# Alternating tiles of one and two experts, later masked adds, one select for two heads, and two buffer pools at the end

## The chip, the cores and the metric

The kernel runs on one core of a Trainium2 chip. Its time is the device time of one execution in microseconds (us). Three executions of the kernel before took 1357.25, 1357.31 and 1363.54 us, so the median is 1357.31 us. A fourth execution was recorded by the profiler; it took 1360.14 us, of which 1358.3 us lie between its first and its last instruction (its span).

The engines are named as in the profile: PE is the matrix engine (TensorE), DVE is VectorE, ACT is ScalarE, POOL is GpSimd and SP is SyncE, which here does nothing but start transfers (DMAs). Each engine has its own queue of instructions and takes them strictly in their order.

## The reference

The input is 2048 rows of 512 numbers. What is computed, in float32, is

```python
xn = layernorm(x)
out = x + attention(xn) + ffn(xn)

# attention: 16 heads, two score maps each (32 maps of width 16), rotary q and k
s = einsum('bthd,bshd->bhts', q, k) * scale      # causal
a = softmax(where(mask, s, -1e30))
attn = irfft((rfft(a1 @ v) - lam * rfft(a2 @ v)) * filt)   # a Gaussian filter along the rows
attn = rms_norm(attn per head) * (1 - LAMBDA_INIT) @ Wout

# ffn: 8 experts of width 352, the best two for every row, and a shared expert of width 704
y_all = einsum('eti,eih->eth', silu(h) * g, w2)
ffn = sum(y_all[topk] * topk_w) + silu(x @ sw1) * (x @ sw3) @ sw2
```

Both softmax maps are divided by their own sums before the second is subtracted from the first. The filter runs over all 2048 rows, so it can start in earnest only when the attention of every row is there.

## The kernel before, in words

**Stages.** From 0 to about 235 us: layer norm, q, k, v, the gate and the routing. From 235 to 600 us: attention, with the shared expert's products strewn in between. From 600 to about 1240 us: attention, with the routed experts' tiles strewn in between. From 1240 us: `ending()`, which applies the filter as matrix products, normalizes, projects with Wout, adds up and stores.

**Order.** In the attention stage all five engines run in the order in which the program writes the instructions; in `ending()` all but SP do. Nothing is rearranged by a scheduler. So the place of a line in the program is its place in its engine's queue.

**Attention.** Heads are taken in 8 groups g of two. In a group the four blocks of 512 queries are taken from the last, qc=3, to the first, qc=0; such a block of a group is a `Chunk`. A chunk's units (up to 512 columns of both maps of one head against 128 keys) go through `scores` (PE, L822, into `ps_s`), the exponential (ACT, L835, into one of 8 buffers `pt`), for units on the diagonal a causal select (POOL, L840), `values` (PE, L862, into `ps_o`), and `added` (DVE, a copy at L876 for the first unit of a head and adds at L879 after that), which keeps the running sums `sum0` and `sum1`. The units that hold diagonal blocks are called masked; the qc=0 chunk has masked units only, five of them, which give two copies and six adds. Four units make one iteration of the loop at L1029; a group has 17 iterations, of some 7.1 us each.

When the last values of a chunk are through, it is `closing`. In the next iteration PE first computes its row sums from `sum0` and `sum1` (`ps_sum`, L888), then transposes its outputs and its sums (`ps_ot` L900, `ps_st` L901), and DVE takes the reciprocals (`rcp`, L903 and L906) and multiplies (`o_n`, L908). An iteration later POOL writes the difference of the two maps into `vd` (L917). `folded` (L922 to L970) prepares a finished group for the filter in some thirty small adds, on POOL for all groups but the last, on DVE for the last one.

On DVE an iteration writes, in this order: the reciprocals and `o_n` of a chunk that closes, the copies and adds of unmasked units among the iteration's first two, the work on the experts' side mixed with one add at a time of the other two, and at last the adds of the iteration's masked units.

**Experts.** The rows sent to the 8 experts are cut into tiles of 128 rows, 34 of which run here. 28 tiles (numbers 0 to 27, `NP`) belong to one expert, 6 tiles (28 to 33) hold 64 rows each of two experts. `experts()` is a generator; each `work()` of the loop above lets it write one piece. For a tile it writes: `xT` (the rows transposed, L165), the first half of the up product with tanh (`xh`, L180, L190, L191), the second half (`xg`, L180, L197), the hidden rows turned back (`ps_u` L206, `uT` L208 and L209) and the down product (`xy`, L216), stored to `ys` at L228. There are two places for an expert's weights, `w_sb[0]` and `w_sb[1]`, each with an up part `wu` (1408 KB) and a down part `wd` (768 KB). Halves of tiles are counted by n, and the half n uses place n % 2; a tile of one expert takes one place, a tile of two experts takes both. When `xg` of a tile is written, SP starts the transfer of the up weights for two halves later into the places that this frees, and behind `xy` likewise for the down weights. After the last tile come the weights of the shared expert (`wex[NX]`, `wex[NX + 1]`), which the last 128 rows still need: `wh<-kept` at L246 and `wy` at L284.

**The end.** `ending()` takes its buffers from the pool `tp` (two of each kind), which lies where pools of the attention stage lay before. Among them are `ws` (L256, the shared expert's hidden values), `res` (12 buffers, loaded with the input's rows, to which POOL's DMA queue adds the shared and the routed outputs by accumulating transfers), `diff`, `first`, and `y_sb`, through which the shared expert's last output goes to `ysh[15]`. Its order on PE: the `wh` products, `ps_r` (L1141, from `vd`), the `ps_z` products (L1141), then 16 times transposes (L1262) and projection (L1270).

Of the kernel before, what the change touches and what calls it, by code (L numbers as in the profile page):

```python
# [19 lines left out]
P = 128  # L20
# [25 lines left out]
NR = NS - 2  # L46

NP = (T * TOP // HALF - NX) // 2
WUP = NE * 2 * FI
WCOL = WUP + NF * E  # L50
CONVS = 23
# [16 lines left out]
def block_kernel(  # L68
# [527 lines left out]
    def middle(general):  # L596


        with ExitStack() as pools:
# [29 lines left out]
            def experts():  # L629
# [45 lines left out]
                xT, late = transposed(xr.pop(0)), None  # L675
                yield 0.6

                sets = [[j] if j < NP else [2 * j - NP, 2 * j - NP + 1] for j in range(NR)]
                halves = [2 * j + i for j in range(NR) for i in range(len(sets[j]))]

                def places(j, part):
                    return [w_sb[n % 2][part] for n in sets[j]]

                def tile_down(j, uT):
                    return places(j, 1), uT, ys[j * P : (j + 1) * P, :], wcol[:, j : j + 1]

                for j in range(NR):
                    if j > 0:
                        late = tile_down(j - 1, turned_back(u))
                    half = up_first(places(j, 0), xT)  # L690
                    yield 2.9 if late else 2.4
                    u = up_third(places(j, 0), xT, half)
                    if j + 2 < NR:
                        xr.append(rows_of(j + 2))
                    for n in sets[j]:

                        m = n + 2 - len(halves)
                        es.append(routed(halves[n + 2]) if m < 0 else wex[NX + m : NX + m + 1])
                        fetch_up(es[n + 2], n % 2, nc.sync)
                    yield 2.4  # L700
                    if j + 1 < NR:
                        xT = transposed(xr.pop(0))
                    if late:
                        down(*late)
                        for n in sets[j - 1]:
                            fetch_down(es[n + 2], n % 2, nc.sync)
                    if j == 1:
                        shared.append(True)
                    if late:
                        yield 3.2  # L710
# [46 lines left out]
            def greatest(g, qc):  # L757
# [28 lines left out]
                nc.vector.tensor_copy(shift, ps.rearrange("p t q -> p (t q)"))  # L786
                return shift

            class Chunk:


# [19 lines left out]
                def scores(self, unit):  # L811

                    g, qc = self.g, self.qc
                    if general and not self.probs:
                        self.shift = greatest(g, qc)
                    ps = sps.tile([P, 2, QC], F32, tag="sc", name="ps_s")
                    for h, kb, off, col, w in unit:
                        for s in range(2):
                            r = slice(64 * s, 64 * s + 64)
                            k = keys[2 * g + h, kb // TQ][r, kb % TQ * P : (kb % TQ + 1) * P]  # L820
                            to = ps[:, s, col : col + w]
                            nc.tensor.matmul(  # L822
                                to, k, queries[2 * g + h, qc][r, off : off + w], start=True, stop=not general
                            )
                            if general:
                                r = 64 * h + 32 * s
                                nc.tensor.matmul(
                                    to, ones[r : r + 1, :], self.shift[r : r + 1, off : off + w],
                                    start=False, stop=kb < qc * TQ,
                                )  # L830
                                if kb >= qc * TQ:
                                    nc.tensor.matmul(to[:, :P], identb, mask, start=False, stop=True)
                    pt = pp.tile([P, 2, QC], F32, tag="pt", name="pt")
                    used = slice(min(c for *_, c, _ in unit), max(c + w for *_, c, w in unit))
                    nc.scalar.activation(pt[:, :, used], ps[:, :, used], AF.Exp, scale=SCALE)  # L835
                    for _, kb, _, col, _ in unit:
                        if kb >= qc * TQ and not general:

                            part = pt[:, :, col : col + P]
                            nc.gpsimd.affine_select(  # L840
                                out=part, in_=part, pattern=[[0, 2], [1, P]], compare_op=ALU.is_ge, fill=0.0,
                                base=0, channel_multiplier=-1,
                            )
                    ready = []
                    for h, kb, off, col, w in unit:
                        self.probs[h, kb] = pt[:, :, col : col + w], off
                        if (1 - h, kb) in self.probs:
                            ready.append((self, kb))
                    return ready
# [134 lines left out]
            for c in range(NQC):  # L984
                load_keys(0, c)
                if c == 0:
                    load_queries(0, NQC - 1)
            worked, begun, summed, held = 0.0, -1, 0, []
            todo, closing, closed, shared, ready, folding = [], [], [], [], [], None

            def burst(units):
# [21 lines left out]
            def work():  # L1013
                nonlocal worked
                worked += next(ex, work_all)

            def masked(entry):
                _, c, unit = entry
                return any(kb >= c.qc * TQ for _, kb, *_ in unit)

            def added(entries):

# [6 lines left out]
            for i in range(0, len(stream), 4):  # L1029
                units = stream[i : i + 4]  # L1030
                found = burst(units[:2])
                n, ended = values()
                for c in closing:
                    c.sums()
                    summed += 1
                if n < 2 and not closing:

                    work()
                found += burst(units[2:])
                while todo:  # L1040
                    ended += values()[1]
                todo += found
                for c in closed:
                    c.put(nc.gpsimd)
                    if c.qc == 0:
                        ready.append(c.g)
                closed, closing = closing, ended
                for c in closed:
                    c.finish()
                held, before = [], held  # L1050
                added(before)
                added(u for u in units[:2] if not masked(u))
                later = [u for u in units[2:] if not masked(u)]
                while True:
                    work()
                    added(later[:1])
                    later = later[1:]
                    if worked / (work_all - left) >= (i + 4) / len(stream):
                        break
                added(later)  # L1060
                added(u for u in units if masked(u))
                if any(map(masked, units)) or not shared:
                    steps = 0
                else:
                    steps = 1 if any(map(masked, stream[i + 4 : i + 8])) else 2
                for _ in range(steps):
                    if folding is None and ready:
                        folding = folded(ready.pop(0), nc.gpsimd)
                    if folding is not None and next(folding, 0) == 0:
                        folding = None  # L1070
            for c in closed:
                c.put(nc.gpsimd)
            ended = []
# [17 lines left out]
    def ending():  # L1091

        with tc.tile_pool(name="tail1", bufs=1) as t1, tc.tile_pool(name="tail", bufs=2) as tp, tc.tile_pool(
            name="tail_ps", bufs=4, space=PSUM
        ) as fps, tc.tile_pool(name="conv_ps", bufs=2, space=PSUM) as zps, tc.manual_schedule(
            engines={mybir.EngineType.PE, mybir.EngineType.DVE, mybir.EngineType.Activation, mybir.EngineType.Pool}
        ):
            conv = t1.tile([P, CONVS * P], F32, name="conv")  # L1100
            nc.scalar.dma_start(conv[:, : 11 * P], conv_t[:, : 11 * P])
            nc.scalar.dma_start(conv[:, 11 * P :], conv_t[:, 11 * P :])
            _, _, _, _, (_, _, stored), _ = expert(tp, fps)
            hidden, gated, times, _, result = shared_expert(tp, fps, 2)
            fetch_down(wex[NX + 1 : NX + 2], 1, nc.scalar)
            wo_sb = t1.tile([P, NE, E], F32, name="wo_sb")
            nc.scalar.dma_start(wo_sb, wout.rearrange("(c p) e -> p c e", p=P))
# [8 lines left out]

            def fetched(k, step):
                if step == 0:
                    res = tp.tile([P, E], F32, tag="res", name="res", bufs=12)
                    nc.sync.dma_start(res, query[0, order[k] * P : (order[k] + 1) * P, :])  # L1120
                    came.append(res)
                elif step == 1:
# [27 lines left out]
                return z  # L1150

            def copied(z):
                diff = tp.tile([P, 2, E], F32, tag="diff", name="diff")
                nc.scalar.copy(diff, z)
                return diff

# [23 lines left out]
            zr = pair("ps_r")  # L1180
            product(zr[:, 0, :], [(0, vd[:, 0, :])])
            product(zr[:, 1, :], [(1, vd[:, 1, :])])
            first = tp.tile([P, E], F32, tag="first", name="first", bufs=1)
            nc.scalar.copy(first, zr[:, 1, :])
            z4 = at(0, fold, 2)
            nc.vector.tensor_add(low[:, 0], zr[:, 0, :], first)
# [283 lines left out]
```

## Time and profile before

| what | value |
| --- | --- |
| three executions | 1357.25, 1357.31, 1363.54 us |
| profiled execution: time, span | 1360.14 us, 1358.3 us |
| mean clock granted to PE | 0.994 of full |
| PE busy | 1312.6 us (97% of the span) |
| DVE busy | 1005.4 us (74%) |
| ACT busy | 688.4 us (51%) |
| POOL busy | 626.3 us (46%) |
| PE busy in 235 to 600 us | 363.18 of 365 us |
| PE busy in 600 to 1240 us | 621.11 of 640 us |
| PE busy in 1240 to 1358.3 us | 103.97 of 118.3 us |

The profiled execution is 2.83 us longer than the median of the three others. 45.7 us of its span are without work on PE; 14 us of these lie behind 1240 us and 19 us between 600 and 1240 us. In the profile a name such as `xy<-wd,uT` tells what an instruction writes and reads; a bracket such as `[2.67 <-DMA wu<-in_wex_dram]` says that the engine had been idle for 2.67 us before the instruction and what ended the idle time.

### The profile page before, as it was taken

How to read it: one execution, taken by the hardware profiler on the slowest of the kernel's cores; microseconds unless marked ns; L12 is line 12 of the kernel's file. 1: busy time of each engine (PE TensorE's matmuls, PEld its weight loads, DVE VectorE, ACT ScalarE, POOL GpSimd, SP SyncE). 2: the span in 40 equal slices, each digit the busy share in tenths (PEclk: the TensorE clock that was granted, in tenths of full speed). 3: DMA queues.
4: the chain of work that ended last, by engine and by line, in shares of the span. 5: the costliest groups of instructions: out<-in, count | busy, mean ns of one | idle time of the engine just before them, and what ended most of it. 6: DMA issues, size and time to landing. Idle time of an engine off the chain costs nothing.

```text
span 1358.3 us, 20810 instructions
## 1 busy us (share of the span) xinstructions
PE 1312.6 (97%) x7554; PEld 600.3 (44%) x7554; DVE 1005.4 (74%) x1344; ACT 688.4 (51%) x847; POOL 626.3 (46%) x671
## 2 busy tenths in 40 slices
PE   7999999999999999999999999899999999987998
PEld 3444444334443444445444444344544444443544
DVE  7049883287668778868889986778898788764785
ACT  2311110265656566676666666566676666640221
POOL 0002330012221323235968984778589469421764
PEclk9999999999999999999999999999999999998999
DMA  9406673200211122235665656555565666777997
GB/s 375 171 16 171 201 196 97 89 15 32 75 43 31 40 75 82 74 123 170 190 194 143 226 176 180 181 173 174 185 194 178 210 189 230 262 294 293 175 219 169
DMA packets 75578, 214.29 MB, mean 158 GB/s; under 512 B 12244, under 2 KB 12696, under 8 KB 69576
## 3 DMA queue, kind: packets, MB, share of 16 engines
q1 hardware_dynamic: 62744, 185.68, 41.7%
q0 software_dynamic: 11056, 22.78, 8.6%
q10 hardware_dynamic: 1664, 4.38, 0.9%
q8 instruction: 63, 1.03, 0.3%
q14 instruction: 51, 0.42, 0.1%
HBM read 169.69 MB, written 43.10 MB: 157 GB/s over the span
## 4 chain that ended last, share of the span: by engine, by line
PE 65%; DVE 6%; POOL 5%; DMA 3%; issue 1%; ACT 1%; SPq 0%; DVEq 0%; ACTq 0%; POOLq 0%
PE ps_o L862 16%; PE ps_s L822 12%; PE wh L246 8%; PE xy L216 6%; PE xg L180 5%; PE xh L180 5%; PE wy L284 4%; PE ps_sum L888 2%; DMA wu<-in_wex_dram 2%; POOL pt L840 1%; PE po L1270 1%; DMA wd<-in_wex_dram 1%; DVE sum L879 1%; PE ps_ot L900 1%; PE ps_x L165 1%
## 5 line engine op out<-in xcount | busy, mean ns | idle before, releaser
L879 DVE TENSOR_TENSOR sum<-sum,pt 128x1024 f32<-128x1024 f32 (+3 forms) x576 | 621.4, 1128 | 36.3 <-ACT pt L835 21.6
L835 ACT ACTIVATE pt<-ps_s 128x1024 f32<-128x1024 f32 x544 | 527.3, 1023 | 184.3 <-PE ps_s L822 131.0
L840 POOL TENSOR_SCALAR_AFFINE_SELECT pt<-pt 128x256 f32<-128x256 f32 x256 | 171.0, 693 | 358.7 <-ACT pt L835 357.5
L862 PE MATMUL ps_o<-pt,vd 128*32 128x512 f32 (+3 forms) x2560 | 268.0, 534 | 4.1 <-POOL pt L840 4.1
L822 PE MATMUL ps_s<-qS,kS 64*128 64x512 f32 (+3 forms) x1280 | 203.8, 406 | 2.0 <-DVEq L1335 1.6
L822 PEld LDWEIGHTS ps_s<-qS,kS 64*128 64x128 f32 x1280 | 97.1, 185 | 177.0 <-issue 95.9
L246 PE MATMUL wh<-xnT,wu 128*128 128x512 f32 (+1 forms) x352 | 150.4, 574 | 0.0
L862 PEld LDWEIGHTS ps_o<-pt,vd 128*32 128x32 f32 x2560 | 66.9, 109 | 125.8 <-issue 103.5
L545 PE MATMUL ps_x<-xnT,wqk_sb 128*128 128x512 f32 x256 | 110.5, 593 | 0.0
L498 POOL DMA_INDIRECT who<-pairs,slot x32 | 33.1, 1034 | 165.9 <-DVE pairs L495 104.9
L216 PE MATMUL xy<-wd,uT 128*128 128x512 f32 (+3 forms) x240 | 97.1, 606 | 7.7 <-DVE rcp L903 6.3
L246 PEld LDWEIGHTS wh<-xnT,wu 128*128 128x128 f32 x352 | 64.1, 190 | 72.7 <-issue 56.5
L180 PE MATMUL xh<-wu,xT 128*128 128x352 f32 (+1 forms) x320 | 90.5, 473 | 4.2 <-DMA wu<-in_wex_dram 3.3
L917 POOL TENSOR_TENSOR vd<-o_n 128x128 f32<-128x128 f32 x60 | 62.2, 1057 | 65.6 <-DVE o_n L908 65.5
L180 PE MATMUL xg<-wu,xT 128*128 128x352 f32 (+1 forms) x320 | 88.6, 468 | 0.0
L545 PEld LDWEIGHTS ps_x<-xnT,wqk_sb 128*128 128x128 f32 x256 | 48.4, 190 | 60.6 <-issue 60.6
L284 PE MATMUL wy<-wd,ws 128*128 128x512 f32 x160 | 74.8, 603 | 0.0
L257 DVE SCALAR_TENSOR_TENSOR ws<-ws,wh 128x512 f32<-128x512 f32 (+4 forms) x26 | 16.7, 644 | 73.6 <-ACT ws L256 73.6
L1125 POOL DMA_INDIRECT res<-ys,slot x32 | 54.9, 1715 | 25.3 <-DMA res<-ysh 13.5
L562 ACT CAST hi<-turned 128x1024 fp32r<-128x1024 f32 x16 | 16.7, 1045 | 93.9 <-DVE turned L560 70.9
L180 PEld LDWEIGHTS xh<-wu,xT 128*128 128x128 f32 (+1 forms) x320 | 48.0, 176 | 31.7 <-issue 6.5
L180 PEld LDWEIGHTS xg<-wu,xT 128*128 128x128 f32 (+1 forms) x320 | 46.6, 174 | 34.4 <-issue 14.8
(254 smaller groups left out, 1416.8 us busy)
## 6 DMA issues: line engine op xcount, KB each, us to landing
wu<-in_wex_dram SPq DMA_DIRECT2D x44, 1408.0 KB
wd<-in_wex_dram SPq DMA_DIRECT2D x43, 768.0 KB
kS<-parts_k SPq DMA_DIRECT2D x128, 128.0 KB
qS<-parts_q SPq DMA_DIRECT2D x256, 64.0 KB
ys<-y_sb SPq DMA_DIRECT2D x34, 256.0 KB
parts_q<-hi SPq DMA_DIRECT2D x32, 256.0 KB
parts_k<-hi SPq DMA_DIRECT2D x16, 256.0 KB
parts_k<-turned SPq DMA_DIRECT2D x16, 256.0 KB
```

Source lines behind the costliest of these rows:

```text
L180: nc.tensor.matmul(dst[r, :], xT[:, c, r], w[:, o : o + FI], start=(c == 0), stop=(c == NE - 1), skip_group_check=True,)
L216: nc.tensor.matmul(y[r, :], uT[:m, ic, r], w[:m, ic * E : (ic + 1) * E], start=(ic == 0), stop=(ic == NF - 1), skip_group_check=True,)
L246: nc.tensor.matmul(dst, w_sb[o // WUP][0][:, o % WUP : o % WUP + P], x[:, c, :], start=(c == 0), stop=(c == NE - 1))
L284: nc.tensor.matmul(y, us[i][:, t * P : (t + 1) * P], w_sb[i // NF][1][:, i % NF * E : (i % NF + 1) * E], start=(i == 0), stop=(i == SCH - 1),)
L545: nc.tensor.matmul(ps[:, i, :], wqk_sb[st, qk][:, i, c, :], xnT[:, c, cols], start=(c == 0), stop=(c == NE - 1),)
L822: nc.tensor.matmul(to, k, queries[2 * g + h, qc][r, off : off + w], start=True, stop=not general)
L835: nc.scalar.activation(pt[:, :, used], ps[:, :, used], AF.Exp, scale=SCALE)
L840: nc.gpsimd.affine_select(out=part, in_=part, pattern=[[0, 2], [1, P]], compare_op=ALU.is_ge, fill=0.0, base=0, channel_multiplier=-1,)
L862: nc.tensor.matmul(self.o[r : r + 32, off:], vd[:, kb, v0 : v0 + 32], pt[:, s, :], start=first, stop=self.ended, skip_group_check=True,)
L879: nc.vector.tensor_add(to, to, pt)
L917: eng.tensor_add(vd[:, self.qc * TQ : (self.qc + 1) * TQ, v0 : v0 + 32], self.o_n[:, :, h, 0, :], self.o_n[:, :, h, 1, :],)
L1125: nc.gpsimd.indirect_dma_start(out=came[k], out_offset=None, in_=ys, in_offset=bass.IndirectOffsetOnAxis(ap=slot[:, step - 2, order[k] : o ...
```

## The change

It has four parts.

1. **The order of the tiles.** The tiles 0 to 21, of one expert, come first. Then tiles of two experts and of one expert take turns: 28, 22, 29, 23, and so on to 33, 27. Before, all tiles of one expert came first and the six of two experts last. The last tile is now one of one expert, in place 1, so that place 0 is free one tile earlier for the up weights of `wex[NX]`. `fetch_down(wex[NX : NX + 1], 0)` behind the last tile stands as it did, and the loop now asks for the same weights one time more.
2. **The masked adds.** In an iteration in which a chunk is closing, the adds of the masked units are no longer written at the iteration's end. They are kept in `waiting` and written in the next iteration, behind the reciprocals and `o_n` and the copies and adds of that iteration's first two units, at the head of the adds that are mixed with the experts' work. These are now written `1 + len(later) // 4` at a time.
3. **One select for two heads.** The last masked unit of a chunk holds the diagonal blocks of two heads; POOL now masks them with one instruction of 128x4x128 where there were two of 128x2x128. There are 224 selects where there were 256.
4. **The pools of the end.** `ws`, `res`, `diff` and `first` come from a new pool `t2`, apart from `tp`; and the shared expert's last `y_sb` is written by ACT (L225) instead of DVE (L227).

```diff
+ORDER = [*range(2 * NP - NR), *(j for i in range(NR - NP) for j in (NP + i, 2 * NP - NR + i))]
...
-                sets = [[j] if j < NP else [2 * j - NP, 2 * j - NP + 1] for j in range(NR)]
-                halves = [2 * j + i for j in range(NR) for i in range(len(sets[j]))]
+                sets, halves = [], []
+                for tj in ORDER:
+                    n = 1 if tj < NP else 2
+                    sets.append(range(len(halves), len(halves) + n))
+                    halves += [2 * tj + i for i in range(n)]
...
                 def tile_down(j, uT):
-                    return places(j, 1), uT, ys[j * P : (j + 1) * P, :], wcol[:, j : j + 1]
+                    tj = ORDER[j]
+                    return places(j, 1), uT, ys[tj * P : (tj + 1) * P, :], wcol[:, tj : tj + 1]
...
-                        xr.append(rows_of(j + 2))
+                        xr.append(rows_of(ORDER[j + 2]))
...
+            def masked(chunk, unit):
+                return any(kb >= chunk.qc * TQ for _, kb, *_ in unit)
...
-                    for _, kb, _, col, _ in unit:
-                        if kb >= qc * TQ and not general:
-
-                            part = pt[:, :, col : col + P]
+                    if masked(self, unit) and not general:
+
+                        cols = [col for *_, col, _ in unit]
+                        if cols == [0, 2 * P]:
+                            looked = [pt.rearrange("p s (h q) -> p (s h) q", h=2)[:, :, :P]]
+                        else:
+                            looked = [pt[:, :, col : col + P] for col in cols]
+                        for part in looked:
                             nc.gpsimd.affine_select(
-                                out=part, in_=part, pattern=[[0, 2], [1, P]], compare_op=ALU.is_ge, fill=0.0,
-                                base=0, channel_multiplier=-1,
+                                out=part, in_=part, pattern=[[0, part.shape[1]], [1, P]], compare_op=ALU.is_ge,
+                                fill=0.0, base=0, channel_multiplier=-1,
                             )
...
                 added(before)
-                added(u for u in units[:2] if not masked(u))
-                later = [u for u in units[2:] if not masked(u)]
+                added(u for u in units[:2] if not masked(*u[1:]))
+                later, waiting = waiting + [u for u in units[2:] if not masked(*u[1:])], []
                 while True:
                     work()
-                    added(later[:1])
-                    later = later[1:]
+                    n = 1 + len(later) // 4
+                    added(later[:n])
+                    later = later[n:]
                     if worked / (work_all - left) >= (i + 4) / len(stream):
                         break
                 added(later)
-                added(u for u in units if masked(u))
+                looked = [u for u in units if masked(*u[1:])]
+                if closing and not general:
+                    waiting = looked
+                else:
+                    added(looked)
...
+            added(waiting)
             for c in closed:
                 c.put(nc.gpsimd)
...
-        with tc.tile_pool(name="tail1", bufs=1) as t1, tc.tile_pool(name="tail", bufs=2) as tp, tc.tile_pool(
-            name="tail_ps", bufs=4, space=PSUM
-        ) as fps, tc.tile_pool(name="conv_ps", bufs=2, space=PSUM) as zps, tc.manual_schedule(
+        with tc.tile_pool(name="tail1", bufs=1) as t1, tc.tile_pool(name="tail2", bufs=2) as t2, tc.tile_pool(
+            name="tail", bufs=2
+        ) as tp, tc.tile_pool(name="tail_ps", bufs=4, space=PSUM) as fps, tc.tile_pool(
+            name="conv_ps", bufs=2, space=PSUM
+        ) as zps, tc.manual_schedule(
...
-            _, _, _, _, (_, _, stored), _ = expert(tp, fps)
-            hidden, gated, times, _, result = shared_expert(tp, fps, 2)
+            _, _, _, _, (_, _, stored), _ = expert(tp, fps, by_scalar=True)
+            hidden, gated, times, _, result = shared_expert(t2, fps, 2)
...
-                    res = tp.tile([P, E], F32, tag="res", name="res", bufs=12)
+                    res = t2.tile([P, E], F32, tag="res", name="res", bufs=12)
...
-                diff = tp.tile([P, 2, E], F32, tag="diff", name="diff")
+                diff = t2.tile([P, 2, E], F32, tag="diff", name="diff")
...
-            first = tp.tile([P, E], F32, tag="first", name="first", bufs=1)
+            first = t2.tile([P, E], F32, tag="first", name="first", bufs=1)
```

More of the change, by code (lines that the diff above doesn't have):

```diff
@@ L987, in middle @@
                     load_queries(0, NQC - 1)
-            worked, begun, summed, held = 0.0, -1, 0, []
+            worked, begun, summed, held, waiting = 0.0, -1, 0, [], []
             todo, closing, closed, shared, ready, folding = [], [], [], [], [], None
@@ L1015, in work @@
                 worked += next(ex, work_all)
-            def masked(entry):
-                _, c, unit = entry
-                return any(kb >= c.qc * TQ for _, kb, *_ in unit)
             def added(entries):
@@ L1060, in middle @@
                 added(later)
-                added(u for u in units if masked(u))
-                if any(map(masked, units)) or not shared:
+                looked = [u for u in units if masked(*u[1:])]
[3 more added lines that the diff above has]
+                    added(looked)
+                if looked or not shared:
                     steps = 0
                 else:
-                    steps = 1 if any(map(masked, stream[i + 4 : i + 8])) else 2
+                    steps = 1 if any(masked(*u[1:]) for u in stream[i + 4 : i + 8]) else 2
                 for _ in range(steps):
```

## The prediction

> **What bounds the kernel now.** I read the page first, then the chain, PE's waits, and the timelines of the places that the change touches.
>
> ```profile
> PE 1312.6 (97%) x7554; PEld 600.3 (44%) x7554; DVE 1005.4 (74%) x1344; ACT 688.4 (51%) x847; POOL 626.3 (46%) x671
> PE 65%; DVE 6%; POOL 5%; DMA 3%; issue 1%; ACT 1%; SPq 0%; DVEq 0%; ACTq 0%; POOLq 0%
> ```
>
> PE is busy 97% of the span and 65% of the chain. The change takes no product from it, so it can only win PE's idle time and lose by making more. PE's waits from 600 to 1250 us list what is to be won:
>
> ```profile
> PE xy L216 <- DVE rcp L903: 6.3, 4, 3.3
> PE ps_o L862 <- POOL pt L840: 4.1, 4, 1.6
> PE xh L180 <- DMA wu<-in_wex_dram: 3.3, 2, 2.7
> PE ps_z L1141 <- DVE vd L1187: 2.6, 1, 2.6
> PE wh L246 <- DMA wu<-in_wex_dram: 2.3, 1, 2.3
> ```
>
> (Columns: total us, times, longest.) Each answers to a part of the change: the first to the masked adds, the second to the select, the others to the order of the tiles and the pools. The timeline of PE shows the waits of the last two parts, all at the end of attention:
>
> ```profile
> 1195.28 4.27 PE L180 MATMUL xh<-wu,xT 128*64 128x352 f32 x14 [2.67 <-DMA wu<-in_wex_dram]
> 1216.87 2.58 PE L180 MATMUL xh<-wu,xT 128*64 128x352 f32 x14 [0.68 <-DMA wu<-in_wex_dram]
> ...
> 1220.56 1.08 PE L888 MATMUL ps_sum<-sum,pick 128*32 128x128 f32 x32 [0.41 <-DVE xtanh L191]
> ...
> 1230.42 5.26 PE L246 MATMUL wh<-kept,wu 128*128 128x128 f32 x32 [2.34 <-DMA wu<-in_wex_dram]
> ...
> 1241.78 1.98 PE L1141 MATMUL ps_r<-vd,conv 128*128 128x512 f32 x4 [0.83 <-ACT y_sb L225]
> ...
> 1249.75 10.52 PE L1141 MATMUL ps_z<-xnT,conv 128*128 128x512 f32 x20 [2.55 <-DVE vd L1187]
> ```
>
> From 1249.75 us on the end is nearly all PE. The xh row of 1195.28 takes 4.27 us for what the row of 1216.87 does in 2.58. Stretches of the timeline with their granted clock (the column behind POOL) say why:
>
> ```profile
> 854.50:858.00 3.50, 3.50 (x4) 1.48 (x5) 3.46 (x5) 0.00 (x0) 2.49 (x3) 0.51 0.25 74
> 1195.80:1199.30 3.50, 3.50 (x12) 1.17 (x8) 0.00 (x0) 0.00 (x0) 0.00 (x0) 0.51 0.56 233
> ```
>
> PE ran at half clock for 3.4 us, which loses 1.7 us. So it did four times (also from 1230.0 and from 1250.5), each time behind an idle time of 3.27, 2.67, 2.34 or 2.55 us; behind idle times of up to 1.58 us it never did.
>
> **Part 2, masked adds: what it wins.** Four xy products waited for a reciprocal that stood behind masked adds on DVE (0.20, 1.43, 3.27 and 1.35 us, at 738, 831, 854 and 1073 us). In the new order the reciprocal comes first: 0.20 + 1.43 + 1.35 = 3.0 us are won. The 3.27 us are dealt with below.
>
> **What it costs: a new wait.** The masked units of a qc=0 chunk are its only units, and they fall into the iteration in which qc=1 closes. So all of the chunk's last copy and six adds are put off into the iteration in which it closes itself, and there PE's ps_sum (L888) needs them. The turn at 503 us shows both engines:
>
> ```profile
> 503.01 0.27 PE L901 MATMUL ps_st<-cst,s_sb 128*128 128x128 f32 x1
> 503.12 2.75 PE L246 MATMUL wh<-xnT,wu 128*128 128x384 f32 x8
> 505.79 0.73 PE L822 MATMUL ps_s<-qS,kS 64*128 64x512 f32 x4
> 506.46 1.92 PE L862 MATMUL ps_o<-pt,vd 128*32 128x512 f32 x16
> 508.20 1.06 PE L888 MATMUL ps_sum<-sum,pick 128*32 128x128 f32 x32
> ```
>
> ```profile
> 499.13 0.69 DVE L876 COPY sum<-pt 128x1024 f32<-128x1024 f32 x1
> 499.73 4.08 DVE L879 TENSOR_TENSOR sum<-sum,pt 128x768 f32<-128x768 f32 x6
> 503.73 0.25 DVE L903 RECIPROCAL rcp<-ps_st 128x16 f32<-128x16 f32 x1
> 504.02 0.23 DVE L906 TENSOR_SCALAR rcp<-rcp,neglam 128x8 f32<-128x8 f32 x1
> 504.29 0.69 DVE L908 TENSOR_TENSOR o_n<-ps_ot,rcp 128x512 f32<-128x512 f32 x1
> 504.89 1.54 DVE L876 COPY sum<-pt 128x1024 f32<-128x1024 f32 x2
> 506.36 0.54 DVE L263 TENSOR_TENSOR ws<-wh,ws 128x384 f32<-128x384 f32 x1
> ```
>
> Let S be the end of ps_st (503.28) and U the start of ps_sum (S + 4.92). Now the copy and the adds, 4.68 us from 499.13 to 503.81, run while PE is on its way to S. Then DVE will stand idle for these 4 us; from S it does the reciprocals and o_n (to S + 1.3), the next group's two copies (to S + 2.75), L263 (to S + 3.2), and only then the 4.68 us: the last add ends at F = S + 7.9. The order of PE is unchanged, so nothing stands in for ps_sum. Six of its 16 products need the last add (0.4 of its 1.06 us), so it ends at F + 0.4 in place of U + 1.06, and PE loses F - U - 0.6 = 2.4 us.
>
> The same at the other turns, F and U counted from S, what stands between the copies and the adds in brackets: 382 us: 8.8, 5.77 (L263 behind wh), 2.4 lost; 615 us: 9.95, 6.60 (L191, which waits for ACT's tanh to S + 4.8), 2.8; 731 and 976 us: 7.9, 4.70 (L197), 2.6 each, and 3.1 if adds run as there before (copy and adds took 5.8 and 5.6 us beside POOL's work): 2.85 taken; 1093 us: 7.4, 5.53, 1.3. At 851 us, where the copy and adds took 8.2 us and xy paid 3.27 and 1.7 us of clock, ps_sum ended at S + 11.6 and will end between S + 7.8 and S + 11.3: 0.3 to 3.8 won; 3.0 taken, because POOL's write of vd and folding lie beside part of the adds. The last group has no such turn: its adds stand as before. Sum: 2.4 + 2.4 + 2.8 + 2 x 2.85 + 1.3 = 14.6 lost, 3.0 won.
>
> Of five waits of 2.4 us and more, some cost half clock too: 5 x 1.7 = 8.5 us if all, 0 if none, because ps_sum's products trickle between the adds and cut the idle time into pieces of a microsecond, and such pieces cost nothing before. The totals are nearest to the idle times that cost four times of four: I take 6.
>
> The Trainium skill ("TensorE: Matmul & The Clock Gate", "HAM oscillation") says that PE should have no idle gaps over about 3.4 us. By that rule, read as it stands, none of the new waits would cost clock and the sum below would be 6 us lower. The rows above show half clock behind gaps of 2.3 to 2.7 us, so here the rows decide.
>
> Behind these turns the second reciprocal comes 2.9 us after F, and two xy (736 and 981 us) wait 0.5 us each: 1.0. At a turn from qc=2 to qc=1 buffers of pt come free later, 0 to 2 us at each of eight; exponentials are ahead there by two units, so I take 0 and keep the rest for the range.
>
> **Part 3, the select.** POOL has 32 selects fewer. The 4.1 us of ps_o waits hang on the last selects of a turn, and two of 0.4 us become one of 0.7 to 0.8: 0 to 4.1, I take 1.0 won.
>
> **Parts 1 and 4, the end.** Products per tile stay the same (16 xh records in 2.52 us for two experts, 8 in 2.37 for one; xy 2.73 and 2.58). In the new order, tile 32 (two experts) finds one place long filled, tile 33 needs one place only, and the shared weights are asked for a tile earlier. So 2.67 + 0.68 + 0.41 us of waits go, and 1.7 of clock: 5.5 won. From the last ps_st (1224.85) to ps_r PE took 16.9 us. Now: xy 2.73, ps_u 0.5, wh at full clock 3.6, xy 2.58, y_sb 0.7 = 10.1, if the down weights of tile 33 are there. SP starts them behind up weights and the ys store at some 1226; 1223 to 1238 moved 4.4 MB here, 0.29 MB/us, so 1.44 + 0.26 + 0.77 MB end near 1232 to 1234, 1 to 3 us late. Taken 11.4: 5.5 won (between 2 and 7). POOL's and SP's queues hold the same transfers, the six res loads now ahead of these weights (1.5 MB, 5 us, released near 1214); that is the lower end. From ps_r to the second ps_z 8.0 us become 5.4, since ws waited 5.39 us on ACT for the y_sb store to give its buffer back: 2.6 won, and 1.6 of clock. y_sb on ACT: 0.7 us, beside PE, 0. Sum 15.2, between 6 and 18.
>
> **The sum.** +14.6 - 3.0 + 6.0 + 1.0 - 3.0 - 1.0 - 15.2 = -0.6 us. The profiled execution had 1360.1 us, so this one would have 1359.5; the median of the runs lies 2.8 us lower: 1356.7. No change.
>
> **Rivals.** (a) Faster: the waits at ps_sum cost as little as the one at 1093 us (1.3 each, 7.8 for 14.6) and no clock: 12.8 less, 1344. For it: ps_sum's pieces. Against it: DVE's queue is written, and the turn at 503 us leaves no room. (b) Slower: the put-off adds run beside POOL. At 851 us copy and adds took 8.2 us beside folding, for 4.68; 3.5 us more at 382, 503, 615 and 1093 us, 3.25 at 731 and 976, 2.7 at 851 make 23: 1380. From a slowing of 1.1 us a turn on it is slower by 0.5%. For it: POOL writes vd and folds in the iteration behind the reciprocals, where the adds now lie. Against: before 600 us POOL does not fold; half of it, 1368, is likelier. (c) The end doesn't do what it says: weights late by 5 us more, res loads in the way, ps_z still waiting. 15.2 becomes 5.5: 1366.
>
> **Chances.** Within 0.5% (6.8 us, about what a measurement of this kernel can tell from no change): 0.41, the forecast, alone 1350 to 1363. (a) 0.27, faster. (b) 0.20 and (c) 0.12: slower, 0.32. The range of 1344 to 1372 leaves out the far ends of (a) and (b).
>
> **What the next profile would show.** ps_sum waiting for the copy or adds of sum (now L889 and L892) six times, 1 to 3 us each, one of the largest groups of PE's waits; DVE idle some 4 us before these reciprocals; the granted clock at half behind several. No xy waiting for rcp at 831, 854 and 1073 us. At the end no xh or wh waiting for wu, and ps_r some 11 us behind the last ps_st. I would be wrong if ps_sum doesn't wait, if adds are slowed at every turn, or if ps_r waits for weights.

## The result, and the profile after

The changed kernel is slower. Four executions took 1401.29 to 1408.02 us, median 1404.18; the kernel before, run beside it, had a median of 1359.84 us. The ratio is 1.0326 (95% interval 1.0282 to 1.0369). The forecast was 1356.7 us with a range of 1344 to 1372; the result lies 32 us beyond it. The profiled execution took 1408.02 us, with a span of 1406.3 us, 48.0 us more than before.

The page of the changed kernel, busy times and chain:

```profile
PE 1328.6 (94%) x7554; PEld 605.8 (43%) x7554; DVE 1001.9 (71%) x1343; ACT 689.2 (49%) x848; POOL 616.7 (44%) x639
...
PE 60%; DVE 8%; DMA 5%; POOL 4%; issue 2%; ACT 2%; SPq 0%; DVEq 0%; ACTq 0%; POOLq 0%
```

PE does the same number of products and is busy for 16.0 us more. Some 10 us of that are products at half clock, by an estimate from the records of the granted clock: PE is busy for 34.0 us in stretches of half clock, against 13.2 before, and half of the difference is lost. It is idle for 32.0 us more (span less busy time: 77.7 us, 45.7 before). What it waited for between 235 and 1300 us (total us, times, longest):

```profile
PE xy L218 <- DMA wd<-in_wex_dram: 28.9, 3, 10.3
PE ps_sum L901 <- DVE sum L892: 12.1, 21, 1.0
PE ps_s L831 <- ACT pt L844: 5.0, 15, 0.4
PE xh L182 <- DMA wu<-in_wex_dram: 3.5, 1, 3.5
PE ps_o L875 <- POOL pt L853: 2.1, 3, 1.4
```

The second row was forecast. The first, three waits for down weights and the largest group by far, was not: two of them lie in the middle of the last stage, and of the third, at the last tile, 1 to 3 us had been forecast. The 6.3 us of xy waiting for rcp have gone.

To see where the 48 us arose, the same instruction can be looked up in both timelines: the end of ps_st, once per turn, then the first ps_r, the start of the second group of ps_z products (at 1249.75 us before), and the end. The difference of the two times grows as follows (places by the time before):

| stretch of the kernel before | time added, us |
| --- | --- |
| start to 983 us (up to the last turn of the sixth group) | +21.3 |
| 983 to 1093 us | +25.9 |
| 1093 to 1156 us | +6.5 |
| 1156 to 1225 us (the last ps_st) | -6.1 |
| 1225 us to ps_r | +4.6 |
| ps_r to the second ps_z | -2.7 |
| second ps_z to the end | -1.6 |
| sum | +48.0 |

**The masked adds, at the turn that the prediction used.** PE of the changed kernel:

```profile
508.37 0.27 PE L914 MATMUL ps_st<-cst,s_sb 128*128 128x128 f32 x1
...
513.55 0.61 PE L901 MATMUL ps_sum<-sum,pick 128*32 128x128 f32 x12
514.84 0.41 PE L901 MATMUL ps_sum<-sum,pick 128*32 128x128 f32 x4 [0.68 <-DVE sum L892]
515.97 0.41 PE L901 MATMUL ps_sum<-sum,pick 128*32 128x128 f32 x4 [0.72 <-DVE sum L892]
516.58 0.63 PE L901 MATMUL ps_sum<-sum,pick 128*32 128x128 f32 x12 [0.19 <-DVE sum L892]
```

and DVE:

```profile
508.68 0.26 DVE L916 RECIPROCAL rcp<-ps_st 128x16 f32<-128x16 f32 x1 [4.11 <-PE ps_st L914]
508.97 0.23 DVE L919 TENSOR_SCALAR rcp<-rcp,neglam 128x8 f32<-128x8 f32 x1
509.31 0.69 DVE L921 TENSOR_TENSOR o_n<-ps_ot,rcp 128x512 f32<-128x512 f32 x1
509.92 1.55 DVE L889 COPY sum<-pt 128x1024 f32<-128x1024 f32 x2
511.38 0.55 DVE L265 TENSOR_TENSOR ws<-wh,ws 128x384 f32<-128x384 f32 x1
511.85 0.68 DVE L889 COPY sum<-pt 128x1024 f32<-128x1024 f32 x1
512.45 6.34 DVE L892 TENSOR_TENSOR sum<-sum,pt 128x768 f32<-128x768 f32 x8
```

DVE stands idle for 4.11 us until ps_st ends at 508.64, as forecast, then does everything at once. The last products of ps_sum start at 516.58, 7.9 us behind ps_st; the prediction had the last add end at 7.9. The turn costs 2.6 us (forecast 2.4).

**The down weights.** The first of the long waits, PE, then SP's transfers ahead of it:

```profile
1058.67 1.07 PE L218 MATMUL xy<-wd,uT 128*64 128x512 f32 x2
1068.88 5.38 PE L218 MATMUL xy<-wd,uT 128*64 128x512 f32 x10 [9.13 <-DMA wd<-in_wex_dram]
```

```profile
1038.45 1.50 SPq L148 DMA_DIRECT2D wu<-in_wex_dram  x2
1039.99 8.49 SPq L745 DMA_DIRECT2D qS<-parts_q  x8
1048.53 2.18 SPq L733 DMA_DIRECT2D kS<-parts_k  x4
1050.81 1.82 SPq L230 DMA_DIRECT2D ys<-y_sb  x1
1052.88 0.37 SPq L151 DMA_DIRECT2D wd<-in_wex_dram  x1
1054.31 0.33 SPq L148 DMA_DIRECT2D wu<-in_wex_dram  x1
```

The two-expert tile needs both places. The place that the one-expert tile before it had used comes free with that tile's xy, at 1044.8 us, and is needed at 1059.7. SP can ask for the weights only behind the next turn's queries and keys, at 1052.9, and they are there at 1068.9: 16 us for 768 KB. Stretches of the same time (columns: length; PE, PEld, DVE, ACT, POOL busy; granted clock; mean busy share of the 16 DMA engines, where a packet counts whole in the stretch in which it starts, so that a share can pass 1; GB/s):

```profile
1050.00:1053.00 3.00, 3.00 (x15) 1.47 (x12) 1.51 (x2) 1.69 (x2) 2.75 (x6) 1.00 0.12 43
1056.00:1060.00 4.00, 3.75 (x51) 2.13 (x43) 1.59 (x4) 2.68 (x4) 1.49 (x4) 1.00 1.02 331
1064.00:1069.00 5.00, 0.12 (x2) 0.12 (x4) 4.79 (x6) 0.00 (x0) 4.68 (x6) 0.51 0.15 58
```

From 1050 to 1053 us and again from 1064 to 1069 us the DMA engines are busy to 0.12 and 0.15 of sixteen, which is the work of about two. In the first stretch the packet records hold little else than packets of 2048 bytes, the rows of keys and queries. So in the second half of PE's wait nearly all DMA engines are idle, and two are behind. This gave the theory for the experiments: a load of keys (kS, 128 KB, written with a leading dimension of two copies of the same 32 rows) goes to two DMA engines only, and what comes behind it on them, a sixteenth of the weights each, waits. The packet records of the weights themselves agree. The load of down weights behind this wait is 128 packets of 6144 bytes, one for each row of wd. 112 of them were done by 1058.8 us, before PE needed them. The last 16, two runs of eight, started at 1065.4 and 1066.6 us, just behind the last packets of 2048 bytes (1065.3 and 1066.5 us), and ended by 1068.4 us.

PE's clock was at half from 1064.1 to 1074.3 us, and for 10.2 us around each of the two other long waits.

### The profile page after: what moved, and what is told of

The parts are those of the page before. It is cut to its first block, busy times and chain, and to the rows that moved or that the text cites. A ratio compares the mean times of both kernels' runs of the same rounds, so it can differ in the third digit from the quotient of the medians.

```text
span 1406.3 us, 20716 instructions
## 1 busy us (share of the span) xinstructions
PE 1328.6 (94%) x7554; PEld 605.8 (43%) x7554; DVE 1001.9 (71%) x1343; ACT 689.2 (49%) x848; POOL 616.7 (44%) x639
## 4 chain that ended last, share of the span: by engine, by line
PE 60%; DVE 8%; DMA 5%; POOL 4%; issue 2%; ACT 2%; SPq 0%; DVEq 0%; ACTq 0%; POOLq 0%
PE ps_o L875 15%; PE ps_s L831 11%; PE wh L248 8%; PE xy L218 6%; PE xh L182 5%; PE xg L182 5%; PE wy L286 4%; DVE sum L892 3%; DMA wd<-in_wex_dram 3%; PE ps_sum L901 2%; PE po L1287 1%; DMA wu<-in_wex_dram 1%; PE ps_ot L913 1%; PE ps_x L167 1%; PE ps_u L208 1%
## 5 line engine op out<-in xcount | busy, mean ns | idle before, releaser
L853 POOL TENSOR_SCALAR_AFFINE_SELECT pt<-pt 128x256 f32<-128x256 f32 (+1 forms) x224 | 161.5, 745 | 390.7 <-ACT pt L844 389.1
L831 PE MATMUL ps_s<-qS,kS 64*128 64x512 f32 (+3 forms) x1280 | 208.6, 410 | 7.1 <-ACT pt L844 5.0
L218 PE MATMUL xy<-wd,uT 128*128 128x512 f32 (+3 forms) x240 | 104.5, 650 | 28.9 <-DMA wd<-in_wex_dram 28.9
L930 POOL TENSOR_TENSOR vd<-o_n 128x128 f32<-128x128 f32 x60 | 67.3, 1140 | 91.6 <-DVE o_n L921 91.6
L916 DVE RECIPROCAL rcp<-ps_st 128x16 f32<-128x16 f32 x32 | 8.3, 259 | 95.1 <-PE ps_st L914 95.0
L227 ACT ACTIVATE y_sb<-xy,wcol 128x512 f32<-128x512 f32 x34 | 23.4, 689 | 93.0 <-PE xy L218 93.0
L218 PEld LDWEIGHTS xy<-wd,uT 128*128 128x128 f32 (+3 forms) x240 | 37.1, 188 | 70.6 <-issue 48.1
```

Of the source, the lines that this page charges most:

```text
L218: nc.tensor.matmul(y[r, :], uT[:m, ic, r], w[:m, ic * E : (ic + 1) * E], start=(ic == 0), stop=(ic == NF - 1), skip_group_check=True,)
L831: nc.tensor.matmul(to, k, queries[2 * g + h, qc][r, off : off + w], start=True, stop=not general)
L853: nc.gpsimd.affine_select(out=part, in_=part, pattern=[[0, part.shape[1]], [1, P]], compare_op=ALU.is_ge, fill=0.0, base=0, channel_multip ...
L930: eng.tensor_add(vd[:, self.qc * TQ : (self.qc + 1) * TQ, v0 : v0 + 32], self.o_n[:, :, h, 0, :], self.o_n[:, :, h, 1, :],)
```

## The experiments

Time and ratio are against the kernel before on the same chip, intervals at 95%. Shifts within a run are differences to the timeline of before, as in the table above.

**One part at a time.** Four kernels, each the kernel before with one piece of the change (the first has part 2 only, the second part 1, the third parts 3 and 4).

> Only the masked adds are put off; tiles, selects and pools as before. The profile of the changed kernel shifts by 21 us up to the turn at 983 us, with ps_sum waiting for adds and four stretches of half clock behind these waits. If the masked adds alone make that (theory), this kernel takes 18 to 24 us more than before, some 1375 to 1381 us, with ps_sum waiting for sum in six or seven turns. Rival: the shift comes in part from the new tile order or the select, then less than 12 us more.

Measured: 1385.41 us, ratio 1.0185 (1.0157 to 1.0212), 25 us more: the theory, at the top of its range and a little over. ps_sum waited 12.6 us for sum in all, ps_s 5.8 us for ACT. 21 of the 25 us were there by 983 us.

> Only the order of the tiles is changed. Theory: xy of a two-expert tile waits about 9 to 10 us twice for its down weights behind 1050 us, and these waits hold PE at half clock, together 20 to 27 us more in the middle; at the end some 3 to 6 us are won: 1372 to 1382 us. Rival: in the changed kernel the weights are late only because the masked adds moved the turns against the tiles; then xy does not wait for wd here, or for less than 5 us, and the time is 1350 to 1358.

Measured: 1391.61 us, ratio 1.0234 (1.0206 to 1.0261), 31 us more. So the tile order is slow by itself, and more than expected. Its longest waits, PE from 235 to 1300 us:

```profile
PE xy L218 <- DMA wd<-in_wex_dram: 17.2, 2, 8.8
PE xh L182 <- DMA wu<-in_wex_dram: 10.3, 2, 6.8
PE xy L218 <- DVE rcp L916: 6.2, 4, 3.3
PE xy L218 <- DVE xnT L975: 5.1, 1, 5.1
```

The up weights are late too, and the last tile's xy waits 5.1 us (the instruction of DVE that is named had long been done; SP asks for this tile's down weights right behind the xy before it). Until 983 us this kernel has no shift beyond 1.1 us.

> Only the select for two heads and the two pools of the end. Theory: the res loads and ws no longer wait for the buffers' release, ps_z comes sooner (2 to 5 us), the select wins 0 to 2 us: 1351 to 1357 us. Rival: the earlier res loads stand on the queue ahead of the last tile's weights, which come later, and the time is the same or some 3 us longer.

Measured: 1361.29 us, ratio 1.0013 (1.0001 to 1.0025): the rival. ps_z does come 2.7 us sooner and the end another 1.9, but on the way to ps_r 6.9 us are lost:

```profile
1240.40 1.94 PE L218 MATMUL xy<-wd,uT 128*64 128x512 f32 x2 [6.80 <-DMA wd<-in_wex_dram]
```

The parts alone cost 25, 31 and 1 us, 57 in all, and the whole change 44. They do not add up. One reason can be seen: the order alone has a wait for up weights of 3.5 us at 1013 us that the whole change does not have. Why it is missing there is not shown.

> The masked adds are put off as in the change, but not those of the first block of queries (qc=0), whose sums are needed in the next iteration. Theory: ps_sum waits for no add, xy does not wait for rcp at 831 and 1073 us, so 1 to 4 us are won: 1353 to 1357 us. Rival: the adds put off give the buffers of pt back later and PE waits for exponentials (ps_s waiting for ACT) at every turn, 0.7 us or more each: 5 to 15 us more than before.

The edit, against the change:

```diff
-                if closing and not general:
+                if closing and not general and all(c.qc > 0 for _, c, _ in looked):
                     waiting = looked
```

Measured: 1370.75 us, ratio 1.0084 (1.0052 to 1.0115). The theory failed, the rival held. ps_sum waits for nothing, but at the turns PE waits for exponentials, as here at a place where it did not wait before:

```profile
366.41 0.49 PE L831 MATMUL ps_s<-qS,kS 64*128 64x512 f32 x2 [0.25 <-ACT pt L844]
367.33 0.56 PE L831 MATMUL ps_s<-qS,kS 64*128 64x512 f32 x2 [0.42 <-ACT pt L844]
```

This turn costs 1.06 us, the next four of its kind 1.08, 1.84, 1.13 and 1.11, and one more turn (at 623 us) 2.9 us with half clock. The turns at 851 and 1093 us, where xy had waited for rcp, win 0.4 us each, all that remains of the reciprocals' wins.

**What holds the weights, and what holds the masked adds.**

> The new tile order alone, and each load of keys (kS, 64 rows at once from a source that is repeated twice) cut into two loads of 32 rows. Theory: in the run with the order alone, the down weights stand behind keys on two of the sixteen DMA engines, because such a load goes to two engines only and leaves them busy for some 12 us; cut in two, it is spread, xy no longer waits 8 to 9 us twice for wd, nor xh 7 us for wu, and 18 to 26 us of the 31 lost go: 1365 to 1374 us. Rival: SP issues the weights late, because it is held at the queries' loads; then four loads more make it later still, xy waits 8 us or more as before, and the time is 1388 us or more.

The edit beside the new order:

```diff
-                        nc.sync.dma_start(
-                            k[64 * s : 64 * s + 64, :].bitcast(F32),
-                            src.unsqueeze(0).to_broadcast([2, 2 * D, QC]),
-                        )
+                        for rep in range(2):
+                            r = 64 * s + 32 * rep
+                            nc.sync.dma_start(k[r : r + 2 * D, :].bitcast(F32), src)
```

Measured: 1355.16 us, ratio 0.9964 (0.9953 to 0.9975): all of the loss gone, more than expected. SP does stay at its loads as long, and longer, yet the weights are in time (the second two-expert tile still waits for them, for 0.5 us). SP, and PE's first two-expert xy, which does not wait:

```profile
1019.24 8.67 SPq L744 DMA_DIRECT2D qS<-parts_q  x8
1027.94 3.68 SPq L735 DMA_DIRECT2D kS<-parts_k  x8
1031.72 0.37 SPq L230 DMA_DIRECT2D ys<-y_sb  x1
1032.34 1.03 SPq L151 DMA_DIRECT2D wd<-in_wex_dram  x1
1034.19 0.34 SPq L148 DMA_DIRECT2D wu<-in_wex_dram  x1
```

```profile
1037.92 2.80 PE L218 MATMUL xy<-wd,uT 128*64 128x512 f32 x12
```

The weights asked for at 1032.3 are used at 1039, 7 us later, against 16 in the changed kernel. With the order alone the same load was asked for at 1037.7 and needed at 1044.2, as little ahead as here, and was there only at 1053.0. So it was not SP's lateness and not the sum of bytes, but how the keys were spread.

> The kernel before with the keys' loads cut in two and nothing else, the control for the runs that have this cut. Theory: in the order before, the weights that meet the keys' loads are asked for two tiles ahead and nobody waits for them, so the cut changes nothing: 1355 to 1361 us, within 0.3% of before. Rival: spreading the loads is a gain of its own, 4 us or more less.

Measured: 1360.23 us, ratio 1.0007 (0.9993 to 1.0021). The cut by itself changes nothing; in the old order nobody waited for what stands behind the keys.

> The whole change with the keys' loads cut in two. Theory: the two waits of 9 to 10 us for wd and the wait of 3.5 us for wu go with their half clock (some 25 us), while the masked adds' part (some 20 us) stays and the last tile's xy still waits for wd behind the res loads: 1374 to 1385 us. Rival: with the weights in time the waits at ps_sum are absorbed too: below 1370.

Measured: 1381.13 us, ratio 1.0160 (1.0142 to 1.0178), 23 us less than the change as it was, and within the theory's range. At 983 us its shift is 21.2 us, as in the change; from there to 1093 us it loses another 3.2 us where the change lost 25.9. The last tile's xy still waits 8.2 us.

> The masked adds are put off, but written right behind o_n, ahead of the copies and adds of the iteration's first two units. Theory: at the qc=0 turns the last add then ends some 6 us behind ps_st in place of 7.4 to 10, so ps_sum waits 0 to 0.7 us a turn in place of 2.5 or more, the half clock there goes, and buffers of pt come free 1.5 us sooner: 1358 to 1368 us, against 1385 with the adds behind the copies. Rival: what costs is that the adds are late at all, and the buffers' release moves from one unit to another: still 1375 us or more.

The edit, against the change (order, selects and pools are those of before):

```diff
                 added(before)
+                added(waiting)
+                waiting = []
                 added(u for u in units[:2] if not masked(*u[1:]))
-                later, waiting = waiting + [u for u in units[2:] if not masked(*u[1:])], []
+                later = [u for u in units[2:] if not masked(*u[1:])]
```

Measured: 1365.42 us, ratio 1.0041 (1.0020 to 1.0062). Of the 25 us, 19 hang on the place behind the copies. Two of its waits:

```profile
PE ps_sum L901 <- DVE sum L892: 3.3, 8, 0.9
PE xh L182 <- DVE rcp L916: 3.3, 2, 1.9
```

ps_s waits for ACT no more than before (0.2 us). This speaks for buffers of pt as what held the exponentials, since only the order of the adds that free them was changed. It does not show it: no run has a ninth buffer, which would test it alone.

**The end, and a version that wins.**

> Of the change only the pools are kept, and res stays in the old pool: ws, diff and first come from the new one, y_sb is written by ACT. Theory: ps_z comes 2 to 3 us sooner and without half clock (1.7 us), and no res load stands ahead of the last tile's weights, so that xy there does not wait 6.8 us as with both select and pools changed: 3 to 6 us less than before, 1352 to 1357 us. Rival: the res loads are not what held these weights; xy waits 5 us or more for wd and the time is that of before.

The edit of the pools, against the change (order, adds and selects are those of before):

```diff
-                    res = t2.tile([P, E], F32, tag="res", name="res", bufs=12)
+                    res = tp.tile([P, E], F32, tag="res", name="res", bufs=12)
```

Measured: 1354.83 us, ratio 0.9969 (0.9957 to 0.9982): the theory. The 2.7 us at ps_z stay won, and xy at the last tile waits 1.4 us in all. So the early res loads had delayed the last tile's weights (the select, the only other difference to the run of parts 3 and 4, has no part in them). The pool for ws, with diff, first and y_sb on ACT, is a gain; the one for res is a loss.

> Not alternating: 26 tiles of one expert, then the six of two, then the last two of one expert; with the keys' loads cut in two, the select for two heads, and the pools as in the run with res in the old pool. Masked adds as before. Theory: the weights of the last tiles are asked for two tiles ahead, so the waits for wu and wd between 1190 and 1240 us go with their stretches of half clock (5 to 10 us), and ps_z as above: 1343 to 1352 us. Rival: two-expert tiles need their weights one tile ahead wherever they stand and now meet the keys' loads of the last group: waits for wd of 5 us or more there, and 1360 us or more.

The edit of the order, against the change:

```diff
-ORDER = [*range(2 * NP - NR), *(j for i in range(NR - NP) for j in (NP + i, 2 * NP - NR + i))]
+ORDER = [*range(NP - 2), *range(NP, NR), NP - 2, NP - 1]
```

Measured: 1345.89 us, ratio 0.9898 (0.9874 to 0.9921), the fastest here. With two one-expert tiles last, their weights are asked for two tiles ahead: from the last ps_st to ps_r it gains 8.5 us on the kernel before.

> The fastest version so far (26 tiles of one expert, six of two, two of one) with the keys' loads as they were. Theory: only the first of the two-expert tiles now meets keys' loads, those near 1080 us, so one wait for wd or wu of 5 to 10 us with half clock comes back: 1352 to 1362 us, against 1346. Rival: the weights' place in the order of the tiles does not matter there: 1344 to 1348.

Measured: 1354.07 us, ratio 0.9960 (0.9946 to 0.9975). One turn, at 1156 us, takes 6.9 us more with waits for up weights, so the keys' cut is worth 8 us here, although it was worth nothing in the old order.

## Why the prediction was wrong

**The tile order: the step that failed.** The prediction costed the order in the middle at nothing ("Products per tile stay the same") and looked for weights only at the end. It named SP's queue there and passed over it at 1050 and 1100 us, where the new order puts two-expert tiles among the keys' loads of the last group. The changed kernel lost 25.9 us there and 4.7 of the 6.5 us behind it, at the wait for wu. The trace of before had both facts. A load of keys keeps about two DMA engines busy: behind the last one, asked for at 1084.9 us, SP's queue kept 12.4% of sixteen engines busy from 1086 to 1089 us (queue, kind: packets, MB, share). And the first two-expert tile came only after it:

```profile
q1 hardware_dynamic: 50, 0.10, 12.4%
```

```profile
1084.85 2.37 SPq L727 DMA_DIRECT2D kS<-parts_k  x4
```

```profile
1121.24 2.59 PE L180 MATMUL xh<-wu,xT 128*64 128x352 f32 x16
```

A one-expert tile's weights are asked for two tiles ahead, which hid the loads everywhere else.

The Trainium skill ("DMA: Bandwidth & Descriptors", "Rules for kernel authors") states that the slowest dimension that is not of size 1 decides over how many of the 16 engines a DMA is split, and names a leading broadcast of c copies as a case that is confined to at most c engines. This fits: a share of 0.12 of sixteen engines, about two, in the stretch above, and the wait gone once the leading dimension of two was cut. Which engines they were, no view here shows.

**The masked adds: the turns right, a term put at nothing.** At the qc=0 turns the forecast losses were 2.4, 2.4, 2.8, 2.85, 2.85 and 1.3 us without clock; measured with clock 3.2, 2.6, 4.4, 4.5, 3.6 and 1.8, and at 851 us 2.6 won (3.0 forecast). Half clock came behind four of these turns, 6.8 us (6 forecast); some 4 us of it lie within the six figures, which without it add up to about 16 us, for 14.6 forecast. What failed is the sentence on pt, "exponentials are ahead there by two units, so I take 0": behind five closings of a qc=2 chunk PE lost 1.06 to 1.12 us each at four and 1.7 us at 615 us, some 6 us in all. At the two turns where a win of 2.8 us by the reciprocals had been forecast, the masked adds alone won 0.4 us each. Over this part the prediction had 15.6 us; the masked adds alone took 25.

**The end: half right.** Forecast were 5.5 won up to the last ps_st (6.1 measured), 2.6 and clock behind ps_r (2.7, then 1.6 to the end), and 5.5 won between, where 4.6 were lost. That term, with a stated range of 2 to 7 us won, had the wrong sign: the last tile's weights were not 1 to 3 us late but 9.45. (Its rate was a little low as well: 4.73 MB moved from 1223 to 1238 us, not 4.4, which makes 0.7 us at most.) The runs part the wait: 5.1 us come from the order itself (the weights are asked for only behind the xy before, also without the res loads). The rest I put down to the early res loads, which without the order make a wait of 6.8 us. How they delay the weights is open: the loads stand on SP's queue, and while the weights moved, from 1282 to 1288 us, transfers of POOL's queue took another 47% of the time of the DMA engines.

```profile
1288.01 5.18 PE L218 MATMUL xy<-wd,uT 128*128 128x512 f32 x6 [9.45 <-DMA wd<-in_wex_dram]
```

**The select** was costed at 1.0 us won. ps_o waits 2.1 us for POOL in the changed kernel, 2.7 with the masked adds alone and the old selects, and 4.1 in the run of parts 3 and 4, as before. So the select won nothing that can be seen.

**The rivals.** (b) named the right sign for a wrong reason: the adds were never slowed by 3.5 us as before at 851 us (by some 1.2 us at 731 and 1.0 at 851, nothing at 503 and 976). (c), the late weights, had the mechanism at the end, and its range stopped at one tile. The range took its width from costs that were listed; a whole stretch that was not looked at had none.

## What to carry to other kernels

When work is reordered, look up for every transfer how far ahead it is asked for in the new order and what stands before it on its queue and its DMA engines, over the whole stretch that is reordered, not only at the places that waited before. Here a DMA whose slowest dimension had two entries loaded two of sixteen engines and held up what stood behind it by its backlog on those, which a mean GB/s or the sum of bytes does not show. And an operation put off behind another can cost twice if its result is needed early: once in the engine that reads it, and once through the buffers that it frees late.

## What the runs showed of the hardware

**Half clock behind short and broken idle time.** Before the half-clock stretch at 391.7 us, PE's idle time was three pieces of 0.70, 0.72 and 0.2 us; a stretch before and the stretch itself:

```profile
386.00:391.60 5.60, 3.99 (x52) 1.67 (x44) 5.39 (x9) 2.20 (x3) 0.00 (x0) 1.00 0.13 50
391.60:395.10 3.50, 3.50 (x12) 2.13 (x9) 2.92 (x6) 1.94 (x2) 0.41 (x1) 0.51 0.12 41
```

The prediction had taken such pieces as a reason to count less than all. They count: four turns with 1.6, 1.7, 1.8 and 2.8 us of idle time in pieces had half clock behind them; three with 0.9, 1.5 and 1.6 us did not. The gap of about 3.4 us that the Trainium skill ("TensorE: Matmul & The Clock Gate", "HAM oscillation") gives as the limit is far above these; here the measurement decides. At one place, 1.9 us of idle time around 755 us, the clock fell in several runs (from 756.6 or so) and not in the profile of before or in the two runs that cut the keys' loads and leave the pools, with the same instructions; that turn then took 1.4 to 1.6 us more.

**Long waits cost more than themselves.** Around each of the three waits of 9 to 10 us the clock is at half for 10.2 us, three times the 3.4 us of a short stretch, of which 4.3 to 5.4 us lie behind the wait, under work.
